# Experts' shares by broadcast transfers instead of selector matmuls, in a two-layer attention and mixture-of-experts kernel

## The chip, the cores and the metric

The kernel runs on one core of one Trainium2 chip. The metric is the device time of one launch in microseconds (us); lower is better. A core has five engines that each work through a queue of their own, in order: TensorE (PE, matmuls; PEld is its weight load), VectorE (DVE), ScalarE (ACT), GpSimd (POOL) and SyncE (SP, which here only issues DMAs). They wait for each other by semaphores. The on-chip memory has 128 partitions; a matmul's result lands in one of 8 PSUM banks, which only PE, DVE and ACT reach. All data are fp32.

## The reference, cut to what matters

The input `x` is 64 batches of 128 rows of 128 numbers. Four layers are added to it one after the other: an attention over 248 keys, a mixture of 8 experts of which each row uses two (its "FFN" of layer 0), a second attention over 120 keys, and a second mixture. The change is in the second mixture, which is computed for all 8 experts and then weighted:

```python
logits = xf @ Wg.T + bg                                   # [rows, 8]
top_gates, top_idx = jax.lax.top_k(logits, 2)
top_gates = jax.nn.softmax(top_gates, axis=-1)            # the two shares of a row
h = jax.nn.gelu(einsum('nd,erd->enr', xf, W1), approximate=False)   # R = 64 per expert
eout = 2.0 * einsum('enr,edr->ned', h, W2)
out = sum(top_gates[:, :, None] * take(eout, top_idx))    # added to x
```

A row's output is thus the sum over the experts of share times `h W2`, where six of the eight shares are zero. The kernel multiplies `h` by the share before it multiplies by `W2`.

## The kernel before

The work is in groups of `GB` = 4 batches, 16 groups in all. The launch has three stages: the first attention with the first router beside it (to about 640 us), the first mixture's tiles (to about 955 us), and the second attention with the second mixture beside it (to the end). The change touches the last stage.

In the second attention, `attention(1, ...)`, one pass of the loop at L553 handles one batch `it`, each step for a batch that is further back. A pass does, in this order (L595 to L612): the values of batch `it-3` (L475) and their copy `ov` (L484); the rounds (L442), which hold the maxima of batch `it` (one matmul per bank at L407, reduced on DVE at L414) and the scores of batch `it-2` (L430) with their exponentials on ACT (L438); then one piece of the experts (`aside.piece`); then the preparation of the next group (`prep`); the output steps `out3`, `out2`, `out4` (L504, L491 with DVE's L495 and L497, L511); the shift of batch `it-1` (transposes at L459, then DVE's L462, which the scores of the next pass need); `out5` (L516) and the statistics for the last norm (L112, L113); and the gathers on POOL for later batches (L1364, L1376). Within one engine this written order is kept: PE, ACT, DVE and POOL are scheduled by hand (`ORDERED`, L16). SP is not in that set in this stage: its order is the scheduler's.

The preparation of group g+1 is spread over the four passes of group g (L354): keys (`prep_k`, L202 and L207) and then `prep_heads` in pass 1, values (`prep_v`, L214 and L221) and the norm's transposes (`prep_x`) in pass 2, queries (`prep_q`, L292 with ACT's L295 and L301) in pass 3. `prep_heads` (L309 to L315) is four DVE multiplications of 128x480 (L313) which make, from the keys, the copies `k4` that the next group's maxima read.

The experts of one group are a generator, `experts` (L1408), of four pieces, so that one piece goes into each pass. Piece 1 (in the pass where `prep_v` stands too) turns the shares of four batches (`gates`, 32 columns per batch of which 8 are used) with one transpose (L1417) and copies the result to `gT` on ACT (L1419); then, for each of four chunks c of two experts each, a matmul into a bank (L1424) and a Gelu on ACT into `hT` (L1427). Piece 2 makes, by 16 matmuls with a constant `select` (L1434; the hardware runs each as two passes, so 32 in the records), the shares of each batch spread over the 128 rows of a chunk, in four banks, and multiplies `hT` by them on DVE (L1439, four instructions, one per batch). Pieces 3 and 4 multiply by `W2` (L1445) and add to `x` (L1450); after piece 4 SP writes the group out (L1452). The exponentials of attention and Gelu need different function tables on ACT; each change of function costs an ACT_TABLE_LOAD, put ahead of the first instruction that needs it.

After the last batch `aside.rest` (L1464) runs the pieces that are left, with nothing of attention beside them: that part is called the tail here.

Of the kernel before, what the change touches and what calls it, by code (L numbers as in the profile page):

```python
# [8 lines left out]
F32 = mybir.dt.float32  # L9
I32 = mybir.dt.int32  # L10
AF = mybir.ActivationFunctionType
ALU = mybir.AluOpType
# [6 lines left out]
GB = 4  # L19
NG = B // GB  # L20
S = 128
# [7 lines left out]
E = 8  # L29
# [15 lines left out]
def transformer_kernel(ctx, tc, a, out):  # L45
    nc = tc.nc

    const = ctx.enter_context(tc.tile_pool(name="const", bufs=1))
# [4 lines left out]
    for g in range(NG):  # L53
        t = resid.tile([S, GB, D], F32, name=f"x_{g}", tag=f"x_{g}")
# [17 lines left out]
    def load_const(name, shape, src):  # L72
        t = const.tile(shape, F32, name=f"c_{name}", tag=f"c_{name}")
        nc.sync.dma_start(t, src)
        return t
# [109 lines left out]
    for s in range(2):  # L185
        k = keep.tile([128, NV, GB, KF + KC], F32, name=f"k2_{s}", tag=f"k2_{s}")
# [14 lines left out]
    def keys_of(w, src, g, n0, pk):  # L201
        nc.tensor.matmul(  # L202
            pk[:, : GB * n0], lhsT=w["wk"], rhs=src.rearrange("d b k -> d (b k)"),
            start=True, stop=True,
        )
        for v in range(NV):
            nc.scalar.activation(  # L207
                K2[g % 2][:, v, :, 0:n0], pk[:, : GB * n0].rearrange("p (b k) -> p b k", b=GB),
                AF.Identity, bias=w["bk"][:, v : v + 1], scale=kmask[:, v : v + 1],
            )  # L210
# [21 lines left out]
    def attention(layer, w, norm, first, aside):  # L232
# [5 lines left out]
        with ExitStack() as es:  # L238
# [37 lines left out]
            def mtile():  # L276
                return banks.tile([128, 512], F32, name="bank", tag="bank")

            def prep_x(g):
                xnT = work.tile([D, GB * S], F32, name="xnT", tag="xnT", bufs=1)  # L280
                norm.turned(normed.pop(g), mtile(), xnT)
                xnTs[g] = xnT
                q4s[g] = work.tile([128, GB, NS, S], F32, name="q4", tag="q4", bufs=3 if first else 2)
                if not first:
                    qfs[g] = work.tile([128, GB, S], F32, name="qf", tag="qf")
# [20 lines left out]
            def prep_k(g):  # L306
                keys_of(w, src[g], g, n0, mtile())

            def prep_heads(g):  # L309

                k4s[g] = work.tile([128, NS, GB, KC], F32, name="k4", tag="k4")
                for s in range(NS):
                    nc.vector.tensor_scalar(  # L313
                        k4s[g][:, s], k2[g % 2][:, s // 2], hmask[:, s : s + 1], None, ALU.mult
                    )  # L315

            def prep_v(g):
                values_of(w, src[g], g, n0, mtile())
# [20 lines left out]
            def prep(it, half):  # L339

                g, j = it // GB + 1, it % GB
                if not first:
                    if g == 1:
                        if (j, half) == (0, 0):
                            prep_k(1)
                            prep_v(1)
                        elif (j, half) == (0, 1):
                            prep_x(1)
                        elif j == 1:
                            prep_q(1, half)  # L350
                            if half:
                                prep_heads(1)
                    elif g < NG:
                        pieces = (  # L354
                            (), (lambda: prep_k(g), lambda: prep_heads(g)),
                            (lambda: prep_v(g), lambda: prep_x(g)),
                            (lambda: prep_q(g, 0), lambda: prep_q(g, 1)),
                        )[j]
                        if half < len(pieces):
                            pieces[half]()  # L360
                    return
                if half == 0 and it < GB - 1:
                    prep_batch(it + 1)
                if (it, half) == (0, 1):
                    prep_v(0)
                    norm_of(1)
                if (it, half) == (1, 1):
                    biased(0)
                if (it, half) == (2, 1):
                    prep_x(1)  # L370
                if (it, half) == (3, 0):
                    prep_q(1, 0)
                    prep_q(1, 1)
                if (j, half) == (3, 1):
                    if g + 1 < NG:
                        prep_x(g + 1)
                elif g >= NG:
                    return
                elif j == 0 and it:
                    prep_q(g, half)  # L380
                elif (j, half) == (2, 0):
                    prep_v(g)
                elif (j, half) == (2, 1):
                    prep_k(g)
# [134 lines left out]
            def norm_of(g):  # L519
                if g < NG:  # L520
                    normed[g] = norm.normed(g)
                    biased(g)
# [262 lines left out]
    hbm = ctx.enter_context(tc.tile_pool(name="hbm", bufs=1, space=bass.MemoryType.DRAM))  # L785
    xs = hbm.tile([E * CAP, ROW], F32, name="xs", tag="xs")
    ys = hbm.tile([NTL * TT, D], F32, name="ys", tag="ys")
    place = ctx.enter_context(tc.tile_pool(name="place", bufs=1))
    at = place.tile([S, B, 2], I32, name="at", tag="at")
    posns = place.tile([S, 2, B], F32, name="posns", tag="posns")  # L790
# [536 lines left out]
    nc.sync.dma_start(row_number, a["row_number"])  # L1327
    steps256 = load_row("steps256", CAP // TT)
    tiles = load_const("tiles", [1, NA], a["tiles"])
    select = load_const("select", [128, 4, 128], a["select"])  # L1330
    lw2 = load_const("lw2T", [128, 4, D], a["lw2T"].rearrange("(c p) d -> p c d", p=128))
    with tc.manual_schedule(engines=ORDERED):
        for _ in range(B - 2):
# [8 lines left out]
    class Aside1:  # L1342
# [65 lines left out]
        def experts(self):  # L1408


            for g in range(NG):
                while not self.ready:
                    yield
                of, gates = self.ready.pop(0)
                assert of == g
                pt = self.mtile()[:, :S]
                nc.tensor.transpose(pt, gates.rearrange("p b e -> p (b e)"), ident)  # L1417
                gT = self.pool.tile([128, S], F32, name="gT", tag="gT", bufs=1)
                nc.scalar.copy(gT, pt)  # L1419
                xnT = self.xnTs.pop(g)  # L1420
                hT = self.pool.tile([128, 4, GB * S], F32, name="h1", tag="h1", bufs=1)
                for c in range(4):
                    ph = self.mtile()
                    nc.tensor.matmul(  # L1424
                        ph, lhsT=lw1[:, c * 128 : (c + 1) * 128], rhs=xnT, start=True, stop=True
                    )
                    nc.scalar.activation(hT[:, c, :], ph, AF.Gelu)  # L1427
                yield

                pg = [self.mtile().rearrange("p (c t) -> p c t", c=4) for _ in range(GB)]  # L1430
                for c in range(4):
                    for j in range(GB):
                        r = slice(32 * j, 32 * j + 32)
                        nc.tensor.matmul(  # L1434
                            pg[j][:, c, :], lhsT=select[r, c, :], rhs=gT[r, :], start=True, stop=True
                        )
                for j in range(GB):
                    h = hT[:, :, j * S : (j + 1) * S]
                    nc.vector.tensor_tensor(h, h, pg[j], ALU.mult)  # L1439
                yield  # L1440
                for j0 in range(0, GB, 2):
                    po = self.mtile()[:, : 2 * D].rearrange("p (j d) -> p j d", j=2)
                    for j in range(2):
                        for c in range(4):
                            nc.tensor.matmul(  # L1445
                                po[:, j, :], lhsT=hT[:, c, (j0 + j) * S : (j0 + j + 1) * S],
                                rhs=lw2[:, c, :], start=(c == 0), stop=(c == 3),
                            )
                    x = xg[g][:, j0 : j0 + 2, :]
                    nc.vector.tensor_tensor(x, x, po, ALU.add)  # L1450
                    if j0:
                        nc.sync.dma_start(  # L1452
                            out[g * GB : (g + 1) * GB].rearrange("b p d -> p b d"), xg[g]
                        )
                    yield
# [21 lines left out]
def _laid_out(inp):  # L1477
# [17 lines left out]
    o = {"x": A["x"]}  # L1495
    o["fsideT"] = A["fside_BxSxS_0"].transpose(2, 0, 1)
    c = A["ctx_1024"]
    o["ctxT"] = c.transpose(2, 0, 1)
    k = moved(c.reshape(B * KC, D)).reshape(B, KC, 1, D)
# [32 lines left out]
    o["upper"] = np.triu(np.ones((128, 128), np.float32), 1)  # L1532
    o["ones"] = np.ones((128, 128), np.float32)
    o["steps256"] = np.arange(CAP // TT, dtype=np.float32) * TT

    t = np.zeros((4, 32, 4, 2, 64), np.float32)
    for e in range(E):
        t[:, e, e // 2, e % 2, :] = 1.0
    o["select"] = t.reshape(128, 4, 128)
    o["tiles"] = np.arange(NA, dtype=np.float32).reshape(1, -1)  # L1540
    o["row_number"] = np.arange(1, 129, dtype=np.float32).reshape(-1, 1)
    o["first_row"] = np.arange(E, dtype=np.float32) * CAP
# [23 lines left out]
```

## Time and profile before

| what | us |
|---|---|
| median of 3 runs (lowest, highest) | 1522.33 (1518.69, 1523.64) |
| the profiled execution, its own time | 1516.1 |
| its span, from the first instruction to the last | 1514.3 |
| PE busy in the span | 1421.0 (94%) |
| DVE busy | 1102.4 (73%) |
| ACT busy | 847.6 (56%) |
| POOL busy | 640.4 (42%) |
| second attention with its experts: first expert matmul (L1424) of groups 0, 11 and 12 | 1071.0, 1435.9, 1461.5 |
| the same of groups 13, 14, 15 (the tail) | 1479.9, 1491.2, 1500.5 |

From group 0 to group 11 a group takes (1435.9 - 1071.0) / 11 = 33.2 us; groups with the router's steps for a pair of groups take about 34.4, the ones between 32.0.

How to read the views: times are counted from the start of the span. A timeline row is start, duration, engine, line, operation, output<-inputs, shapes and count, and in square brackets the engine's idle time before it and what released it. A row of the chain of waits is start, duration, and what the end of the launch was waiting for in that stretch. A row of the windows view gives, for one stretch, its length, each engine's busy time and number of instructions, then the clock granted to TensorE (1 is full), the busy share of the DMA engines, and the GB/s that they moved. PE's busy time is modelled and holds waits inside a group of matmuls.

### The profile page before, as it was taken

The page shows a single profiled execution, that of the slowest core. Times are in us where ns is not written, and L with a number is a line of the kernel's source. Part 1 is how long each engine was busy: PE and PEld are TensorE (multiplying, and loading weights), DVE is VectorE, ACT ScalarE, POOL GpSimd, SP SyncE. Part 2 cuts the span into 40 slices and gives each one's busy share as a digit, 9 for nine tenths or more (in the row PEclk, how much of TensorE's full clock was granted, in tenths as well). Part 3 has the DMA queues.
Part 4 walks back from the last instruction along what each step waited for, and adds up shares of the span by engine and source line. Part 5 has one row for each costly group of instructions (what it writes and reads, how often), then busy time and mean ns, then how long its engine had stood idle before and what let it go on. Part 6 is the DMA issues. An engine that isn't in the chain of part 4 may idle for free.

```text
span 1514.3 us, 42033 instructions
## 1 busy us (share of the span) xinstructions
PE 1421.0 (94%) x16620; PEld 1107.5 (73%) x16620; DVE 1102.4 (73%) x3024; ACT 847.6 (56%) x1740; POOL 640.4 (42%) x1195
## 2 busy tenths in 40 slices
PE   7999999999999999888999999898999999999987
PEld 5777777777777677777888888566666776767665
DVE  6777888888888988455754444687777778787763
ACT  4666666666666666543333333566667566666643
POOL 4123254646465635654001122377546555454210
PEclk9999999999999999999999999899999999999999
DMA  8433333333222221366766667111011111100000
GB/s 201 120 80 80 79 82 96 89 93 94 63 66 60 58 73 40 107 184 202 214 197 199 201 195 205 49 34 34 22 36 29 39 35 32 31 29 23 8 16 22
DMA packets 143719, 133.03 MB, mean 88 GB/s; under 512 B 48546, under 2 KB 126114, under 8 KB 141602
## 3 DMA queue, kind: packets, MB, share of 16 engines
q1 hardware_dynamic: 135330, 113.02, 27.3%
q0 software_dynamic: 8192, 17.32, 3.7%
q8 instruction: 132, 2.16, 0.6%
q14 instruction: 65, 0.53, 0.1%
HBM read 97.32 MB, written 32.97 MB: 86 GB/s over the span
## 4 chain that ended last, share of the span: by engine, by line
PE 69%; DVE 15%; DMA 4%; POOL 4%; ACT 4%; issue 2%; SPq 1%; POOLq 0%; DVEq 0%; ACTq 0%
PE bank L430 11%; PE bank L394 10%; PE bank L475 9%; PE bank L1115 9%; PE bank L1424 4%; PE bank L1445 4%; DVE nm L414 4%; PE bank L1128 3%; DMA q<-xs 2%; PE bank L407 2%; PE bank L214 2%; DVE q L462 2%; PE bank L511 2%; PE bank L681 2%; PE bank L202 2%
## 5 line engine op out<-in xcount | busy, mean ns | idle before, releaser
L414 DVE TENSOR_REDUCE nm<-bank 128x2 f32<-128x496 f32 (+1 forms) x768 | 463.5, 662 | 77.6 <-PE bank L430 61.8
L438 ACT ACTIVATE p<-bank 120x512 f32<-120x512 f32 (+1 forms) x768 | 402.1, 605 | 126.8 <-PE bank L430 123.9
L430 PE MATMUL bank<-q,k 32*120 32x256 f32 (+1 forms) x3072 | 438.1, 399 | 11.4 <-DVE nm L414 5.2
L430 PEld LDWEIGHTS bank<-q,k 32*120 32x120 f32 (+1 forms) x3072 | 293.5, 181 | 56.8 <-DVE nm L414 17.3
L394 PE MATMUL bank<-k,q 32*128 32x248 f32 x2048 | 291.0, 399 | 0.7 <-ACT q L334 0.5
L394 PEld LDWEIGHTS bank<-k,q 32*128 32x128 f32 x2048 | 202.2, 189 | 47.9 <-issue 11.0
L1120 DVE TENSOR_TENSOR p<-p,bank 128x256 f32<-128x256 f32 x213 | 88.0, 420 | 121.0 <-ACT p L1119 120.5
L475 PE MATMUL bank<-p,v 128*32 128x128 f32 (+1 forms) x4096 | 175.6, 275 | 0.2
L407 PE MATMUL bank<-k,qf 32*128 32x480 f32 x512 | 153.8, 602 | 0.8 <-ACT qf L295 0.8
L807 POOL DMA_INDIRECT xs<-xn,at x128 | 129.2, 1009 | 27.9 <-issue 24.3
L1119 ACT ACTIVATE p<-bank 128x256 f32<-128x256 f32 x213 | 81.0, 384 | 98.9 <-PE bank L1115 97.9
L484 ACT COPY ov<-bank 128x256 f32<-128x256 f32 x128 | 48.1, 376 | 143.5 <-PE bank L475 143.4
L475 PEld LDWEIGHTS bank<-p,v 128*32 128x32 f32 (+1 forms) x4096 | 108.8, 109 | 22.8 <-issue 13.7
L1364 POOL DMA_INDIRECT yb<-ys,back x112 | 108.5, 969 | 27.7 <-issue 19.5
L1115 PE MATMUL bank<-q 128*128 128x256 f32 x516 | 118.6, 379 | 1.6 <-ACT q L1106 1.6
L462 DVE SCALAR_TENSOR_TENSOR q<-bank,c_smask,q 128x256 f32<-128x256 f32 x256 | 111.1, 475 | 8.2 <-PE bank L459 7.8
L167 POOL TENSOR_SCALAR xn<-x,mv,rstd 128x128 f32<-128x128 f32 x252 | 110.2, 449 | 7.5 <-issue 1.4
L1115 PEld LDWEIGHTS bank<-q 128*128 128x128 f32 x516 | 94.7, 190 | 13.0 <-ACT q L1106 1.9
L475 PE MATMUL bank<-p,vc 120*32 120x128 f32 x2048 | 103.2, 272 | 0.0
L155 POOL TENSOR_SCALAR rstd<-mv 128x4 f32<-128x4 f32 x32 | 6.3, 198 | 219.9 <-DVE mv L113 123.0
L301 ACT ACTIVATE q<-bank,c_a_bq,c_hmask 128x512 f32<-128x512 f32 x124 | 90.1, 789 | 9.8 <-PE bank L292 9.8
L1157 POOL DMA_INDIRECT kvT<-ys,back x16 | 15.4, 961 | 189.7 <-DMA vc<-xs 114.0
(224 smaller groups left out, 2465.7 us busy)
## 6 DMA issues: line engine op xcount, KB each, us to landing
q<-in_w SPq DMA_DIRECT2D x43, 576.0 KB
vc<-in_w SPq DMA_DIRECT2D x28, 576.0 KB
vc<-in_ctx_v SPq DMA_DIRECT2D x16, 960.0 KB
ys<-zero SPq DMA_DIRECT2D x71, 128.0 KB
k<-in_ctx_k SPq DMA_DIRECT2D x32, 240.0 KB
q<-xs SPq DMA_DIRECT2D x43, 128.0 KB
ys<-q SPq DMA_DIRECT2D x43, 128.0 KB
x<-in_x SPq DMA_DIRECT2D x16, 256.0 KB
```

Of the source, the lines that this page charges most:

```text
L167: nc.gpsimd.tensor_scalar(xn[:, j, :D], xg[g][:, j, :], self.mv[:, b, 0:1], self.rstd[:, b : b + 1], ALU.add, ALU.mult,)
L301: nc.scalar.activation(q4s[g][:, :, s, :], pq.rearrange("p (b q) -> p b q", b=GB), AF.Identity, bias=w["bq"][:, s : s + 1], scale=hmask[:, ...
L394: nc.tensor.matmul(pa[:, u, :], lhsT=q4s[g][r, j, s, :], rhs=k2[g % 2][r, s // 2, j, :], start=True, stop=True,)
L407: lambda: nc.tensor.matmul(pa, lhsT=qfs[g][r, j, :], rhs=k4s[g][r, :, j, :], start=True, stop=True),
L414: nc.vector.tensor_reduce(nm[b % 2].rearrange("q i (a s) -> q a i s", s=16)[:, 2 * ra + v : 2 * ra + v + len(slots) // 2, :, 0], pa.rearra ...
L430: nc.tensor.matmul(pb[:n, v * 256 : (v + 1) * 256], lhsT=k2[g % 2][r, v, j, k0 : k0 + n], rhs=q4s[g][r, j, 2 * v : 2 * v + 2, :].rearrange ...
L438: nc.scalar.activation(ps_[b][:n, c, ra, :], pb[:n], AF.Exp, scale=SCALE)
L462: nc.vector.scalar_tensor_tensor(q, pm, smask[:, v : v + 1], q, ALU.mult, ALU.add)
L475: nc.tensor.matmul(pav[32 * ra : 32 * ra + 32, v * S : (v + 1) * S], lhsT=vs[g % 2][c][:, j, 4 * v + ra, i, :], rhs=p[:n, c, ra, (2 * v + ...
L807: s = nc.gpsimd.indirect_dma_start(xs, bass.IndirectOffsetOnAxis(at[:, j, k : k + 1], 0), xn, None)
L1115: nc.tensor.matmul(ph[:, u, :], lhsT=w[:, c, u * 128 : (u + 1) * 128], rhs=xT, start=True, stop=True)
L1364: nc.gpsimd.indirect_dma_start(y[:, k, b % 2, :], None, ys, bass.IndirectOffsetOnAxis(back[:, b, k : k + 1], 0),)
```

## The change

The shares are no longer made by matmuls. `gT` becomes a part of a new tile `share` (128 x 4 x 512); after the copy on ACT, SP writes its 4 x 8 used rows of 512 B each to a scratch in HBM (`shares_`, [8 experts, 4 batches, 128], two of them in turn), and two further DMAs read it back, each to 64 partitions: every one of these partitions gets, for each chunk c, the 2 KB row of one expert (256 pieces of 2 KB per DMA, 512 KB; together 1 MB). `hT` is then multiplied by `share` chunk by chunk: chunks 0 and 1 on GpSimd, 2 and 3 on VectorE. An exponential of one element, to no use in the result, follows the Gelus on ACT. The constant `select` and its load go. `prep_heads` moves from the second half of pass 1 to just ahead of `prep_v` in pass 2, where it stands behind that pass's maxima in DVE's queue.

```diff
@@ prep, groups from 2 on
                         pieces = (
-                            (), (lambda: prep_k(g), lambda: prep_heads(g)),
-                            (lambda: prep_v(g), lambda: prep_x(g)),
+                            (), (lambda: prep_k(g),),
+                            (lambda: (prep_heads(g), prep_v(g)), lambda: prep_x(g)),
                             (lambda: prep_q(g, 0), lambda: prep_q(g, 1)),
                         )[j]
@@
+    shares_ = [hbm.tile([E, GB, S], F32, name=f"shares_{k}", tag=f"shares_{k}") for k in range(2)]
@@
-    select = load_const("select", [128, 4, 128], a["select"])
+    again = const.tile([1, 2], F32, name="again", tag="again")
+    nc.vector.memset(again, 0.0)
@@ experts
-                gT = self.pool.tile([128, S], F32, name="gT", tag="gT", bufs=1)
+                share = self.pool.tile([128, 4, GB * S], F32, name="share", tag="share", bufs=1)
+                gT = share[:, 3, :S]
                 nc.scalar.copy(gT, pt)
+                there = shares_[g % 2]
+                for j in range(GB):
+                    nc.sync.dma_start(there[:, j, :], gT[32 * j : 32 * j + E, :])
+                for i in range(2):
+                    nc.sync.dma_start(
+                        share[64 * i : 64 * i + 64],
+                        there.rearrange("(c i) j t -> i c (j t)", i=2)[i]
+                        .unsqueeze(0).to_broadcast([64, 4, GB * S]),
+                    )
...
                     nc.scalar.activation(hT[:, c, :], ph, AF.Gelu)
+                nc.scalar.activation(again[:, 1:2], again[:, 0:1], AF.Exp)
                 yield
-                pg = [self.mtile().rearrange("p (c t) -> p c t", c=4) for _ in range(GB)]
                 for c in range(4):
-                    for j in range(GB):
-                        r = slice(32 * j, 32 * j + 32)
-                        nc.tensor.matmul(
-                            pg[j][:, c, :], lhsT=select[r, c, :], rhs=gT[r, :], start=True, stop=True
-                        )
-                for j in range(GB):
-                    h = hT[:, :, j * S : (j + 1) * S]
-                    nc.vector.tensor_tensor(h, h, pg[j], ALU.mult)
+                    (nc.gpsimd if c < 2 else nc.vector).tensor_tensor(
+                        hT[:, c, :], hT[:, c, :], share[:, c, :], ALU.mult
+                    )
                 yield
```

In the changed program SP's queue holds, for a group of the first nine: the four writes; the load of the keys' source `kvT` for a later group (L256), which waits for PE's values of this pass (L214); the two reads; and the output of an older group. From group 9 on there is no `kvT` between. For the last two groups the output of the group before stands behind the first of the four writes. On POOL the two multiplications stand between the gathers of two passes, on DVE where L1439 stood.

More of the change, by code (lines that the diff above doesn't have):

```diff
@@ L1534, in _laid_out @@
     o["steps256"] = np.arange(CAP // TT, dtype=np.float32) * TT
[L1536 to L1539, printed above, removed]
     o["tiles"] = np.arange(NA, dtype=np.float32).reshape(1, -1)
```

## The prediction

> **What bounds the kernel now.** I read the busy table first (PE 94%, but PE's busy time is modelled and holds waits), then the chain of waits in the last stage, which says what was waited for. Two neighbouring groups, cut to the rows that the change touches (start, us, what):
>
> ```profile
> 1178.40 1.28 ACT L438
> 1179.70 0.61 ACT p L438
> 1180.35 1.02 PE bank L1434 x24
> 1181.42 2.48 DVE h L1439 x4
> ...
> 1198.86 1.52 DVE k L313 x4
> ...
> 1212.84 1.28 ACT L438
> 1214.14 0.61 ACT p L438
> 1214.79 1.16 PE bank L1434 x28
> 1215.95 1.06 PE bank L292 x2
> ...
> 1231.38 1.51 DVE k L313 x4
> ```
>
> The first group (1169.5 to 1204.0, 34.4 us, with the router's steps) goes through the table load of ACT, the exponential, the selector matmuls and the four multiplications, and from there to the next L1424 it stays mostly with DVE; L313 is on it. The second (32.0 us) leaves DVE after L1434 and runs along PE; L313 comes back only near the end. So the change works on pieces that do set the end, in both kinds of group. The timeline gives the moments between which the new transfers must fit:
>
> ```profile
> 1170.07 0.30 ACT L1419 COPY gT<-bank 128x128 f32<-128x128 f32 x1
> ...
> 1174.12 0.33 SPq L256 DMA_DIRECT2D kvT<-in_ctxT  x1
> 1174.13 0.76 DVE L221 TENSOR_TENSOR v<-bank,c_a_bv 120x256 f32<-120x256 f32 x2 [3.54 <-PE bank L214]
> ...
> 1178.22 2.35 DVE L414 TENSOR_REDUCE nm<-bank 128x4 f32<-128x480 f32 x4
> ...
> 1181.42 2.48 DVE L1439 TENSOR_TENSOR h<-h,bank 128x512 f32<-128x512 f32 x4 [0.85 <-PE bank L1434]
> ```
>
> Call T the end of the copy to `gT`: 1170.37, and 1204.31 in the second group. DVE is ready to multiply at 1180.57 = T+10.2 (second group 1214.98 = T+10.7), and its next instruction starts at 1183.82 (1218.26).
>
> **The transfers (not in the trace before).** SP issues one DMA per 0.47 us (the first loads: 3.20, 3.67, 4.14), and data move about 0.6 us after the issue. So: four writes issued to T+2.0, landed about T+2.9; then the load of `kvT` at T+3.75 stands ahead of the reads (it waits for PE's L214); reads issued to T+5.0; their data from about T+6.0, behind those of `kvT`. The share is there at T+6.0+D+0.1, D being the data time of 1 MB. The nearest rows (length, then busy times; the last columns are clock, DMA share, GB/s):
>
> ```profile
> 6.30:7.50 1.20, 1.20 (x2) 0.23 (x1) 0.34 (x2) 0.00 (x0) 0.75 (x1) 1.00 1.13 324
> 32.10:34.20 2.10, 2.10 (x30) 1.77 (x32) 1.09 (x3) 0.39 (x2) 0.66 (x1) 0.73 0.26 59
> 1175.00:1176.50 1.50, 1.50 (x26) 1.33 (x30) 0.85 (x4) 0.54 (x1) 1.47 (x2) 1.00 0.75 213
> ```
>
> 324 GB/s is the best stretch (a load of keys): D = 3.2. 59 GB/s is a constant's 512 B row sent to 128 partitions, the only rows of that kind: D = 17.8. 213 GB/s is `kvT`, in pieces of 1,920 B, nearly the 2 KB of the new ones: D = 4.9, which I take, since the size of the piece is what the new transfer shares with it. The share then lands at T+11.0, and at T+9.05 where no `kvT` stands between (groups 9 to 11: reads issued from T+2.9, data from T+4.05).
>
> The Trainium skill ("SBUF — State Buffer", section "Door 1: The DMA port swizzle") says that a transfer to partitions 0 to 63 reaches only half of the ports, 196 GB/s measured for 1 MiB. By it D would be an estimated 5.3, which speaks against halving the partitions; no transfer here goes to 64 of them.
>
> **The multiplications.** Rows: SBUF by SBUF on DVE 0.68 us (L1012, 128x512), on POOL 1.27 (L526, same size). Two each: DVE 1.36 alone; 3.9 if its two stand behind POOL's two (2.54); L313 takes 0.46 alone and up to 0.68 beside POOL's L167, so they do disturb each other. I take one POOL instruction between DVE's two, 2.6, and for POOL 3.2.
>
> The Trainium skill (same page, "SBUF: two separate sides") calls the port pair of the two engines an exclusive lock, also for a VectorE operation with two SBUF inputs against a GpSimd one that reads SBUF. The L313 row agrees with a disturbance, not yet with a full block; the page's end would be 3.9, some 18 us more over the launch than my 2.6.
>
> **Per group in attention.** The multiplication ended at 1183.82. First kind: 1181.37 + 2.6 = 1183.97, +0.15; L313 off its place, -1.5 (in its new place DVE idles 3.5 us ahead of L221, so it costs nothing there; if PE's L214 came 2 us earlier it would): -1.35. Second kind: 1215.31 + 2.6 = 1217.9 against 1218.26, -0.35, and -1.5, since PE, which set this group's end, loses the table load and the selector matmuls (1.28 + 1.16 = 2.4): -1.85. Mean -1.6 in nine groups; in groups 9 to 11, where the share is there before DVE asks, -2.15. Sum -20.9. Three uses of L313 before the first experts: -2. The exponential's table load now stands behind the Gelus, ahead of need; its cover is some 3 us in which ACT waits for PE. POOL idles 7.1 us later in the pass (L155), so its 3.2 and its wait move gathers that have room: 0 taken, 0.5 a group (6) if that room is gone. The constant's removed load and the memset: 0.
>
> **Group 12 and the tail.** Group 12 (`gT` at 1462.1, no `kvT`): share 1471.1, DVE done 1473.7 against 1470.1: +3.6, and 0.9 for POOL, whose multiplications now stand ahead of the last norm (1473.4): +4.5. In the tail nothing of attention lies beside the transfer:
>
> ```profile
> 1480.00:1484.00 4.00, 4.00 (x6) 1.54 (x5) 1.14 (x6) 2.40 (x4) 0.00 (x0) 0.51 0.00 0
> ...
> 1491.18 3.60 PE L1424 MATMUL bank<-xnT,c_lw1T 128*128 128x512 f32 x8
> 1494.71 1.17 PE L1434 MATMUL bank<-gT,c_select 32*128 32x128 f32 x32
> 1496.71 3.84 PE L1445 MATMUL bank<-c_lw2T,h 128*128 128x128 f32 x32 [0.83 <-DVE h L1439]
> ```
>
> A tail group took 9.32 us (1491.07 to 1500.39, from transpose to transpose; 11.46 the first, 9.5 the last). Now: transpose and copy 0.63, share 4.05 + 4.9 + 0.1 = 9.05 (reads issued right behind the writes), 0.1, POOL 3.2, L1445 3.6, 0.1, and a colder PE: after about 3 us without work the clock of L1424 was 0.51 and its eight took 5.61 instead of 3.60, so +2.0 on L1445 (0 to 3.84). Sum 18.7, and 19.1 where an output stands between SP's writes: +7.2, +9.8, +9.6 = +26.6.
>
> **Sum**: -20.9 - 2 + 4.5 + 26.6 = +8.2. The profiled execution took 1516.1 (span 1514.3), so 1524.3; the median of the runs is 1522.33, 6.2 above it: **1530.5**. What the attention gains, the tail gives back.
>
> **Rivals.**
> *A, faster: the share is there when DVE asks, and the two engines don't block each other.* D = 4.1 (256 GB/s) and 1.36 us: first kind ends 1.9 earlier, with L313 -3.4; second kind held by PE at -2.4; 12 groups -34.7, -2, group 12 +2.5, tail +22.2: -12, 1510. From one side alone it decides at D under 4.1 (slope 13 us per us: nine groups, group 12, three tail groups) or at a multiplication under 1.9. For it: 324 GB/s was moved, DVE's 0.68 row. Against it: `kvT` never kept 324 over its transfer, L313's row.
> *B, the reads run like the constants' broadcast.* All pieces come from eight rows of HBM, as there from one. At 59 GB/s, D = 17.8: 12.9 x 13 + 11.5 x 3 (groups 9 to 11) on top, 1734; at 118 GB/s, D = 8.9, 52 + 8 more: 1591. For it: the only broadcast in the trace. Against: pieces of 512 B, and DMA engines busy 26% there, so few bytes per piece may be what made it slow.
> *POOL becomes the bound:* 3.2 us in each group against 7.1 of idle time; at worst 6 us, inside the range. That the table load would stay on the path is excluded by the order: it follows the Gelus there.
>
> **Chances.** Forecast 0.50 (its own range 1518 to 1560: D from 4.1 to 6.5, multiplications from 1.9 to 3.9), A 0.27, B 0.23. The range reaches to A's 1505 (PE's end a little lower than I hold) and B's milder end, 1600. About 0.3% (4.6 us) is what can be told from no change. Faster: A nearly whole, 0.25, and a little of the forecast, 0.05: 0.30. Same: 0.12 of the forecast and A's rest. Slower: 0.58.
>
> **What the profile after would show.** Right: reads landing 10.5 to 11.5 us after the copy; DVE waiting about 0.8 us for them in the first kind; a period of 31 to 32; no ACT table load in the chain ahead of L438; L313 in DVE's idle time before `v`; tail groups near 19 with clock near half on L1445. Wrong: a landing beyond T+13 (B), before T+10.2 (A), multiplications of DVE longer than 2.6 from start to end, or a period that does not fall although DVE ends earlier, since PE then has a bound of its own.

## The result, and the profile after

| | before | changed |
|---|---|---|
| median of 4 runs (lowest to highest), us | 1520.51 (1517.61 to 1523.64) | 1584.83 (1582.58 to 1594.57) |
| span of the profiled execution | 1514.3 | 1585.0 |
| start of the experts to the end (from the first `gT`) | 442.9 | 513.3 |
| groups 0 to 8 | 299.9 | 330.9 |
| groups 9 to 11 | 90.8 | 93.3 |
| group 12 | 18.3 | 24.8 |
| tail, groups 13 to 15 | 33.9 | 64.3 |

The ratio is 1.043, with an interval of 1.0404 to 1.0455. The rows of groups are differences between the ends of the copies to `gT` (L1422 in the changed kernel); the sum forecast -14.4, -6.5, +4.5 and +26.6 for the last four, and -2 ahead of them. So group 12 and the tail came nearly as worked out; the nine groups with `kvT` are 31 us longer instead of 14 shorter, and groups 9 to 11 are 2.5 longer instead of 6.5 shorter.

One of the nine, timeline of the changed kernel (T is 1182.10):

```profile
1181.80 0.30 ACT L1422 COPY share<-bank 128x128 f32<-128x128 f32 x1
1182.12 1.30 SPq L1426 DMA_DIRECT2D shares<-share  x4
1185.53 0.36 SPq L256 DMA_DIRECT2D kvT<-in_ctxT  x1
1186.12 1.24 SPq L1428 DMA_DIRECT2D share<-shares  x2
...
1196.12 0.69 DVE L1445 TENSOR_TENSOR h<-h,share 128x512 f32<-128x512 f32 x1 [4.15 <-DMA share<-shares]
1196.16 1.77 POOL L1445 TENSOR_TENSOR h<-h,share 128x512 f32<-128x512 f32 x1 [4.91 <-DMA share<-shares]
...
1196.73 1.75 DVE L1445 TENSOR_TENSOR h<-h,share 128x512 f32<-128x512 f32 x1
...
1197.89 1.71 POOL L1445 TENSOR_TENSOR h<-h,share 128x512 f32<-128x512 f32 x1
```

The reads are issued from T+4.0 to T+5.3, near the sum's T+5.0, but DVE starts at T+14.0 and not T+11.0: it stood 4.15 us. The chain of waits goes through this transfer for 9.3 us:

```profile
1186.75 9.29 DMA share<-shares
```

The windows view (length; busy times of PE, PEld, DVE, ACT, POOL; clock, DMA share, GB/s) shows the read itself, then what the wait does to PE, then a read in the tail:

```profile
1188.00:1195.50 7.50, 6.27 (x90) 3.99 (x79) 3.86 (x12) 6.05 (x12) 2.72 (x4) 1.00 0.79 165
1194.30:1199.50 5.20, 0.00 (x0) 0.00 (x0) 3.35 (x7) 1.27 (x3) 3.34 (x2) 0.77 0.05 10
1199.50:1203.60 4.10, 4.06 (x23) 2.89 (x23) 3.89 (x13) 1.08 (x2) 3.53 (x5) 0.50 0.14 34
...
1545.50:1549.50 4.00, 0.00 (x0) 0.00 (x0) 0.00 (x0) 0.05 (x1) 0.00 (x0) 0.90 1.02 230
```

In attention the read keeps 165 GB/s with the gathers' transfers among it, and its packets run from 1187.7 to 1195.5, 7.8 us, the longest of the nine (6.5 to 7.8, mean 7.0); in the tail they run 5.1 us. PE has nothing for 5.2 us, since the scores (L430) need DVE's L462, which stands behind the multiplications; and when they come, PE works at a clock of 0.50 for 4 us. The waits from 1071 to 1402 (in all, times, longest) and the tail's timeline:

```profile
PEld bank L430 <- DVE q L462: 49.0, 9, 6.0
...
DVE h L1445 <- DMA share<-shares: 25.5, 7, 4.2
```

```profile
1540.05 0.27 ACT L1422 COPY share<-bank 128x128 f32<-128x128 f32 x1 [4.12 <-PE bank L1419]
...
1543.60 1.24 SPq L1428 DMA_DIRECT2D share<-shares  x2
1551.22 3.44 POOL L1445 TENSOR_TENSOR h<-h,share 128x512 f32<-128x512 f32 x2 [17.05 <-DMA share<-shares]
...
1554.72 5.62 PE L1453 MATMUL bank<-c_lw2T,h 128*128 128x128 f32 x30 [0.88 <-POOL h L1445]
```

5.62 us for thirty L1453 (two more had run ahead of them), where the sum had 3.6 + 2.0; GpSimd 3.44, where it had 3.2. The release came late: the last packet ended at 1550.3, and the multiplications start 0.9 us after it; over all groups this gap is 0.6 to 1.1 us.

### The profile page after: what moved, and what is told of

Its sections match the earlier page's. It is cut to its first block, busy times and chain, and to the rows that moved or that the text cites. A ratio compares the mean times of both kernels' runs of the same rounds, so it can differ in the third digit from the quotient of the medians.

```text
span 1585.0 us, 41284 instructions
## 1 busy us (share of the span) xinstructions
PE 1420.2 (90%) x16108; PEld 1109.0 (70%) x16108; DVE 1116.5 (70%) x2993; ACT 852.1 (54%) x1759; POOL 701.0 (44%) x1227
## 4 chain that ended last, share of the span: by engine, by line
PE 65%; DVE 13%; DMA 11%; POOL 4%; ACT 2%; issue 2%; SPq 1%; POOLq 0%; ACTq 0%; DVEq 0%
PE bank L430 11%; PE bank L394 9%; PE bank L1116 8%; PE bank L475 8%; DMA share<-shares 6%; PE bank L1453 5%; DVE nm L414 4%; PE bank L1129 3%; PE bank L407 3%; PE bank L1437 2%; DMA q<-xs 2%; PE bank L214 2%; DVE h L1445 2%; DMA vc<-xs 2%; PE bank L202 2%
## 5 line engine op out<-in xcount | busy, mean ns | idle before, releaser
L430 PE MATMUL bank<-q,k 32*120 32x256 f32 (+1 forms) x3072 | 454.0, 413 | 60.0 <-DVE q L462 53.1
L430 PEld LDWEIGHTS bank<-q,k 32*120 32x120 f32 (+1 forms) x3072 | 307.5, 188 | 104.3 <-DVE q L462 65.0
L407 PE MATMUL bank<-k,qf 32*128 32x480 f32 x512 | 168.7, 654 | 0.8 <-ACT qf L295 0.8
L1453 PE MATMUL bank<-c_lw2T,h 128*128 128x128 f32 x512 | 82.6, 326 | 44.7 <-POOL h L1445 37.6
L1453 PEld LDWEIGHTS bank<-c_lw2T,h 128*128 128x128 f32 x512 | 75.8, 234 | 63.4 <-POOL h L1445 41.5
L167 POOL TENSOR_SCALAR xn<-x,mv,rstd 128x128 f32<-128x128 f32 x252 | 114.2, 466 | 7.5 <-issue 1.4
L462 DVE SCALAR_TENSOR_TENSOR q<-bank,c_smask,q 128x256 f32<-128x256 f32 x256 | 111.0, 475 | 6.9 <-PE bank L459 6.5
L1445 POOL TENSOR_TENSOR h<-h,share 128x512 f32<-128x512 f32 x32 | 54.5, 1724 | 129.1 <-DMA share<-shares 110.7
```

The costliest lines, as they stand in the source:

```text
L167: nc.gpsimd.tensor_scalar(xn[:, j, :D], xg[g][:, j, :], self.mv[:, b, 0:1], self.rstd[:, b : b + 1], ALU.add, ALU.mult,)
L407: lambda: nc.tensor.matmul(pa, lhsT=qfs[g][r, j, :], rhs=k4s[g][r, :, j, :], start=True, stop=True),
L430: nc.tensor.matmul(pb[:n, v * 256 : (v + 1) * 256], lhsT=k2[g % 2][r, v, j, k0 : k0 + n], rhs=q4s[g][r, j, 2 * v : 2 * v + 2, :].rearrange ...
L462: nc.vector.scalar_tensor_tensor(q, pm, smask[:, v : v + 1], q, ALU.mult, ALU.add)
L1453: nc.tensor.matmul(po[:, j, :], lhsT=hT[:, c, (j0 + j) * S : (j0 + j + 1) * S], rhs=lw2[:, c, :], start=(c == 0), stop=(c == 3),)
```

## The experiments

My theory after the result: the transfers land late, the clock falls in the wait, and what does not touch the shares gains as worked out. The rival: the two engines' multiplications are what costs. The runs were made on several chips, and the chip matters: the kernel before took 1576 on the one of e5 to e8 and 1574 on the one of e9 to e12, but 1519 to 1520 on those of e1 to e4, of e13 to e16 and of e17 and e18. I call these the slower and the faster chips. So e5 to e8 and e10 to e12 are set against the changed kernel on a slower chip (e9; for e5 to e8 it is the other of the two), and times of groups only against such from chips of the same pace.

**e1, e2, e3: the parts without the shares.** Edits to the kernel before; e1 has the first, e2 the second, e3 both:

```diff
-    (), (lambda: prep_k(g), lambda: prep_heads(g)),
-    (lambda: prep_v(g), lambda: prep_x(g)),
+    (), (lambda: prep_k(g),),
+    (lambda: (prep_heads(g), prep_v(g)), lambda: prep_x(g)),
```

```diff
     nc.scalar.activation(hT[:, c, :], ph, AF.Gelu)
+nc.scalar.activation(again[:, 1:2], again[:, 0:1], AF.Exp)
```

> The kernel before with one part of the change alone: the heads' keys (L313) are made ahead of the values in pass 2. My theory: the parts that do not touch the shares gain what the sum gave them, and the loss lies in the transfers. Then this gains 1.5 us in each group with the router's steps and 0.6 to 1.5 in the others, 12 to 18 in all: 1502 to 1509. Rival: attention is held by something else (PE's own length), and L313 only moves the wait: within 5 of 1520.

> The kernel before with another part alone: the exponential of one element behind the Gelus, so that the table load leaves the wait. My theory: DVE waited 0.85 us ahead of the multiplications for PE, which waited for ACT; groups with the router's steps gain 0.85, the others up to 1.28: 10 to 13 in all, 1507 to 1511. Rival: the earlier load only lengthens ACT's queue, within 5 of 1520.

> The kernel before with the two parts together, shares still made by selector matmuls. My theory: the gains add up, since one lies ahead of the multiplications and one behind them: 22 to 31, 1489 to 1498. Rival (PE is the bound of a group): no more than the larger of the two alone.

Measured, beside 1519.35 for the kernel before: 1502.94 (ratio 0.989, 0.986 to 0.991), 1509.14 (0.992, 0.990 to 0.995) and 1495.69 (0.983, 0.980 to 0.986). All three lie in the theory's ranges, and nearly add up. So two parts of the change are worth 24 us, and the shares cost 89.

**e4: no transport.** `self.still` is filled once with 0.25.

```diff
-    share = self.pool.tile([128, 4, GB * S], F32, name="share", ...)
+    share = self.still
...
-    nc.sync.dma_start(there[:, j, :], gT[32 * j : 32 * j + E, :])
-    nc.sync.dma_start(share[64 * i : 64 * i + 64], ...)
```

> The changed kernel without the transport: no writes and no reads of the shares; the tile of shares is filled once with a constant, so the output lacks the real shares. Multiplications, their engines and the order stay. My theory (the loss is the wait for the transfers and the clock that falls in it): groups in attention about 2 us under those of before, the tail groups about 2 us over: 1495 to 1510. Rival (the multiplications on two engines disturb each other, and PE waits for GpSimd's): stays over 1560.

Measured 1501.83 (0.989, 0.985 to 0.992). The rival fell as an explanation of the loss: with both engines multiplying as in the change, 83 of its us are gone with the transport. But groups 0 to 8 took 293.9 us here, where the theory had some 282, and 283.8 with the selector matmuls in their old place (e16); e17 goes after that. One cause shows in the multiplications. A group of e4 in which GpSimd begins first, cut together from DVE's and GpSimd's timelines:

```profile
1106.62 1.28 POOL L1437 TENSOR_TENSOR h<-h,share 128x512 f32<-128x512 f32 x1
1107.21 2.47 DVE L1437 TENSOR_TENSOR h<-h,share 128x512 f32<-128x512 f32 x1
1107.84 1.28 POOL L1437 TENSOR_TENSOR h<-h,share 128x512 f32<-128x512 f32 x1
...
1109.61 0.68 DVE L1437 TENSOR_TENSOR h<-h,share 128x512 f32<-128x512 f32 x1
```

GpSimd's two take no longer than alone, one right behind the other, and DVE's first, started beside them, ends only 0.56 us after GpSimd's second: it was held all the while. In the changed kernel, where both start together, they take turns: 0.69, then 1.77, 1.75 and 1.71, each but the first longer by about as much as was left of the other engine's one.

**e5: `kvT` off SP's queue.**

```diff
-    nc.sync.dma_start(t, a["fsideT" if first else "ctxT"][...])
+    (nc.sync if first else nc.scalar).dma_start(t, a[...][...])
```

> The changed kernel, with the loads of kvT in the second attention issued from ACT's queue at the start of a group's first pass instead of from SP between the writes and the reads. My theory: that load holds the reads back by about 1.7 us and its data another 1, and with the clock that falls in the wait it makes the nine groups 3.4 us longer; without it they run like groups 9 to 11 (32.4 us): 1550 to 1558. Rival (GpSimd's gathers slow the reads, whatever stands on SP): little of it comes back, over 1570.

1594.76 (1.013 of before, 1.009 to 1.016), against 1619.74 for e9: 25 less. Its groups 0 to 8 took 304.9 us against 336.2, and their reads 5.2 to 6.9 us (mean 5.8) against 5.4 to 7.5 (6.9), begun 2 us earlier. The theory's numbers were for a faster chip; as a difference it had 27 to 35, a little more than came.

**e6, e7: reads to all partitions, two repeats outermost.**

```diff
-    for i in range(2):
-        nc.sync.dma_start(share[64 * i : 64 * i + 64], ...)
+    for c in range(4):
+        nc.sync.dma_start(
+            share[:, c, :],
+            there.rearrange("(c i) j t -> i c (j t)", i=2)[:, c]
+            .unsqueeze(1).to_broadcast([2, 64, GB * S]),
+        )
```

> The changed kernel, with the share read back by four DMAs of one chunk each to all 128 partitions (256 KB each, the same 2 KB pieces) instead of two DMAs to 64 partitions each; kvT stays between. My theory: a piece took 84 ns at the head of the read and 171 ns once all 16 DMA engines wrote to one half of the partitions, so with both halves open 1 MB takes near 3 us alone instead of 5.0: tail groups 2 us shorter, groups in attention 2 to 3.5 (clock included): 1548 to 1565. Rival (eight rows of HBM or the gathers are what slows the pieces): 1580 to 1587.

> Both edits of the two runs before this one. My theory: the share lands before DVE asks in all groups of attention, which then run as with no transport (about 2 us under before each), and only the tail and group 12 are left as loss (about +20): 1512 to 1528. Rivals: as the better one of the two alone, 1550 or more, if only one of the two was the cause.

1831.98 and 1831.68 (both 1.162 of before): far on the other side of every expectation. The windows view of e6 within a read:

```profile
1210.00:1216.00 6.00, 1.31 (x14) 0.33 (x6) 0.00 (x0) 2.36 (x5) 1.87 (x2) 0.74 0.13 51
```

A DMA share of 0.13 is two of 16 engines, and 51 GB/s is 25 pieces of 2 KB in a us, each 84 ns long in the records: the pieces were quick, but only two engines had any. The step that stands outermost in this read has two repeats, in the change's own read 64. These two runs say nothing on the halves of the partitions.

**e8: PE kept busy.**

```diff
+    for _ in range(5 if g < 9 else 10 if g > 11 else 0):
+        nc.tensor.matmul(self.mtile(), lhsT=lw1[:, :128], rhs=xnT, start=True, stop=True)
     for c in range(4):
         (nc.gpsimd if c < 2 else nc.vector).tensor_tensor(...)
```

> The changed kernel with matmuls that nobody reads (five of 128x512 in groups 0 to 8, none in 9 to 11, ten from group 12 on) behind the L1437 matmuls' pass, so that PE is not idle while DVE waits for the share. The transfers are unchanged. My theory: of the 3.4 us that a group lost, 1.5 to 1.8 is PE running at half clock after the wait, and about 2 us of each tail group: 1560 to 1568. Rival (the whole loss is the wait itself): 1583 to 1600, the matmuls only adding.

1608.62 against 1619.74: 11 less, though PE does more; the theory had 17 to 25 less and the rival none. Groups 0 to 8 took 326.2 us against 336.2, with a granted clock of 0.99 against 0.90, while DVE started as late as before (T+13.4 to T+14.9, in e9 T+12.9 to T+14.8). The clock is shown as a cause, with 1.1 us a group, net of the added matmuls, instead of the 1.5 to 1.8 that I expected. From the first `gT` on, the profile of e8 is 19 us shorter; ahead of it, where nothing was edited, 7 longer, so the 11 hold a difference between the two chips or executions too.

**e9 and e10: the changed kernel on a slower chip, and the second read on ACT's queue.**

```diff
+    read(nc.sync, 0)
...
     nc.scalar.activation(again[:, 1:2], again[:, 0:1], AF.Exp)
+    read(nc.scalar, 1)
```

> The changed kernel once more, as it is, beside the three of this call, because the kernel before took 1575 in the call before this one against 1520 in the others, and its numbers have to be set against the changed kernel of the same chip: 1.04 of the kernel before.

> The changed kernel with the second of the two reads (to partitions 64 to 127) issued from ACT's queue behind the Gelus instead of from SP; sizes and pieces stay. My theory: a read to 64 partitions is held by that half, 171 ns a piece, so the two halves written at the same time take near 3 us instead of 5.0, and one of them passes kvT: tail groups 2 us shorter, attention's 2 to 3: 25 to 35 less than the changed kernel beside it. Rival (eight rows of HBM set the pace): within 8 of it.

e9: 1619.74, 1.029 of before (1.027 to 1.030), where the faster chip gave 1.043. e10: 1601.22, 18.5 less, all of it in attention: groups 0 to 8 took 312.2 us against 336.2, the tail 65.6 against 63.2. In attention the two reads hardly met: ACT's had passed `kvT` and was nearly done (1166.6 to 1170.1 in one group) when SP's began at 1169.7. In the tail they were issued at the same moment (1548.19 on SP, 1548.20 on ACT), and still their packets ran one after the other, SP's from 1549.6 to 1552.3 and ACT's from 1551.6 to 1554.8, 5.2 us in all. So two queues did not get the two halves written at the same time, and e10's gain is most likely that of passing `kvT`.

**e11: experts in turn over the partitions.** W1 and W2 are laid out to match; same bytes, same 2 KB pieces.

```diff
-    for i in range(2):
-        nc.sync.dma_start(share[64 * i : 64 * i + 64], ...)
+    for c in range(4):
+        nc.sync.dma_start(
+            share[:, c, :],
+            there[2 * c : 2 * c + 2].rearrange("i j t -> i (j t)")
+            .unsqueeze(0).to_broadcast([64, 2, GB * S]),
+        )
```

> The changed kernel with each chunk's two experts laid in turn over even and odd partitions (the weights W1 and W2 are laid out to match), so that a read of one chunk goes to all 128 partitions in 2 KB pieces with 64 repeats as its outermost step, four DMAs of 256 KB. In the run with four DMAs of two repeats of 64 only 25 pieces came per us, each still 84 ns long, so about two DMA engines worked; my theory for that run is that a DMA is dealt to the engines by its outermost step. Then here all engines work, to both halves: 1 MB in 3 us, 20 to 35 less than the changed kernel beside it. Rival 1 (128 partitions in one DMA is what was slow): 1800 or more. Rival 2 (eight rows of HBM set the pace of the pieces): within 8 of the changed kernel.

1549.19 (0.984 of before, 0.982 to 0.985): 70.5 less than e9, twice what I expected. Rival 1 fell, and with it the doubt on e6: 128 partitions are quick when 64 repeats stand outermost. Rival 2 fell too, since the same eight rows of HBM are read. Within a read, and the multiplications by kind (busy, mean ns, idle before):

```profile
1202.50:1205.00 2.50, 2.35 (x25) 1.38 (x18) 2.43 (x9) 1.09 (x2) 2.17 (x3) 1.00 0.99 324
```

```profile
L1445 POOL TENSOR_TENSOR h<-h,share 128x512 f32<-128x512 f32 x32 | 40.1, 1271 | 59.9 <-DMA share<-shares 52.1 <-ACT oT L506 7.5
L1445 DVE TENSOR_TENSOR h<-h,share 128x512 f32<-128x512 f32 x32 | 28.4, 925 | 27.1 <-DMA share<-shares 26.5 <-ACT p L438 0.5
```

The nearest stretch of the changed kernel, with its DMA engines as busy:

```profile
1189.00:1194.00 5.00, 5.00 (x65) 3.21 (x58) 2.91 (x8) 4.23 (x10) 1.91 (x2) 1.00 0.97 200
```

324 GB/s instead of 200. Pieces took 84 ns (median in every group), where the changed kernel's took 84 in the first microsecond of a read and mostly 115 to 180 after it. The whole read of 1 MB is shortened by less, since its four DMAs are issued one after the other: 4.3 to 5.2 us in groups 0 to 8 against 5.4 to 7.5 in e9, and 4.0 to 4.3 in the tail against 5.1 to 5.4. Since the chunks land one after the other, GpSimd also starts before DVE: 1,271 and 925 ns a multiplication, against 1,708 and 1,265 in e9.

**e12: selector matmuls back in groups 12 to 15.**

```diff
+TAIL = 12
...
+    if g == TAIL:
+        nc.sync.dma_start(share[:, 0, :].rearrange("p (c m) -> p c m", c=4), a["select"])
...
+    if g < TAIL:
         for c in range(4):
             (nc.gpsimd if c < 2 else nc.vector).tensor_tensor(...)
+    else:
...
+        nc.tensor.matmul(pg[j][:, c, :], lhsT=select[r, c, :], rhs=gT[r, :], ...)
...
+        nc.vector.tensor_tensor(h, h, pg[j], ALU.mult)
```

> The changed kernel up to group 11; groups 12 to 15 make their shares with the selector matmuls and multiply on DVE as before the change (the selector is loaded into the tile of the shares, which is free then). My theory: group 12 and the tail are half of the loss, 36: 34 to 38 less than the changed kernel beside it. Rival (the end is late because of what attention left behind): under 15 less.

1585.30: 34.4 less than e9, in the theory's range. Tail 33.0 us against 63.1, group 12 18.5 against 24.9.

**e13: the order of landing alone.**

```diff
-    for i in range(2):
-        nc.sync.dma_start(share[64 * i : 64 * i + 64], ...)
+    for h in range(2):
+        for i in range(2):
+            nc.sync.dma_start(share[64 * i : 64 * i + 64, 2 * h : 2 * h + 2, :], ...)
```

> The changed kernel with each of its two reads cut in two by chunks, in the order chunks 0 and 1 of both halves of the partitions, then chunks 2 and 3 of both: GpSimd's half lands first, but every DMA still goes to 64 partitions. My theory for the 70 us that the spread layout gained: most of it is the pace (171 ns a piece when one half is written, 84 when both are), a smaller part that GpSimd and DVE no longer start together (1.7 and 1.2 us a multiplication, 1.27 and 0.68 apart): here pieces stay at 171 ns, and 15 to 30 less than the changed kernel (1.029 of before where before takes 1574). Rival (the order of landing is all of the gain): 55 to 75 less.

On a faster chip: 1557.61 (1.025, 1.022 to 1.029), 27 less than the changed kernel's 1584.83, in the theory's range. Pieces took 112 to 148 ns (medians of the groups), far from e11's 84. Its multiplications:

```profile
L1446 POOL TENSOR_TENSOR h<-h,share 128x512 f32<-128x512 f32 x32 | 39.9, 1268 | 82.5 <-DMA share<-shares 73.6 <-ACT ov L484 5.1 <-ACT qf L295 2.5
L1446 DVE TENSOR_TENSOR h<-h,share 128x512 f32<-128x512 f32 x32 | 24.0, 790 | 58.7 <-DMA share<-shares 58.7
```

1,268 and 790 ns, where the changed kernel had 1,724 and 1,244. So the common landing cost 27 of the 70 or so. In the rest two things are together that no run takes apart: the pace of a read to one half, and e11's landing in four steps instead of two. The two figures are also from different chips, so the split is rough.

**e14, e15, e16: can the transfers be made to pay?** e14 is e11 with e12's edit, e15 adds e5's, e16 is e3 again beside them.

> The spread layout with the selector matmuls back in groups 12 to 15. My theory: its four last groups were 20 us longer than those of the run with the tail undone, so 1529 where before takes 1574 (0.97 of before). Rival (the two edits share their gain): 1540 or more.

> The same with kvT loaded from ACT's queue. My theory: DVE still waited up to 1.4 us between its two multiplications in groups 0 to 8 for the last chunk, since kvT stood ahead; without it 5 to 12 less than the run beside it. Rival (what is left is not the transfer's): within 4 of it.

> Once more the kernel before with the moved keys and the early table load and no transfers, beside the spread layout's best: which of the two ways is better. 0.983 of before. My theory: the spread layout with the tail undone is better by 1% or more, since it takes the selector matmuls from PE and 1.1 us of multiplication from DVE in each group. Rival: equal, attention being bound by what both leave alone.

1507.08 (0.992, 0.989 to 0.994), 1511.52 (0.995, 0.993 to 0.997) and 1495.91 (0.986, 0.984 to 0.989). All three theories fell (e14 came out as its rival had it: the two edits share their gain): the best form of the transfers beats the kernel before and loses to the kernel with the two other parts and no transfers at all, by 11 us; and with the pace right, `kvT` on SP costs nothing that shows. Groups 0 to 8: 296.0, 297.1 and 283.8 us.

**e17, e18: all multiplications on DVE**, without transport (e4's edit) and with e14's.

```diff
-    (nc.gpsimd if c < 2 else nc.vector).tensor_tensor(
+    nc.vector.tensor_tensor(
```

> The run without transport (shares filled once with a constant, so the output lacks the real ones) with all four multiplications on DVE. My theory: there DVE's two multiplications took 3.0 us because GpSimd's, started just ahead, held its first one for 2.1; four of 0.68 on DVE alone take 2.7, and PE no longer waits for GpSimd, so groups with the router's steps fall from 33.4 or 35.2 to about 33, the others stay at 30.5: groups 0 to 8 take 285 to 290 us instead of 293.9, in the tail nothing changes: 0.982 to 0.987 of before. Rival (GpSimd takes work off DVE, as the change would have it): slower than with GpSimd, 0.99 or more.

> The spread layout with the selector matmuls back in groups 12 to 15 and all four multiplications on DVE. My theory: with the transfers landing chunk by chunk DVE multiplies chunks 0 and 1 while 2 and 3 are on their way, so it gains little or nothing over the run with GpSimd (0.992 of before): 0.985 to 0.995, and the kernel before with the two other parts alone (0.983 to 0.986) stays the best. Rival (without GpSimd in it the transfers pay): 0.98 or less.

1510.86 (0.994, 0.992 to 0.996) and 1510.36 (0.994, 0.991 to 0.996). The theory of e17 fell: groups 0 to 8 took 299.9 us, more than with GpSimd (293.9). Four multiplications on DVE took 3.33 us where I had 2.7: they are held by GpSimd's additions of gathered rows too (1.37 us for one that began beside such an addition; mean 848 ns, not 680). The four from PSUM before the change took 2.48, each between 677 and 689 ns, beside GpSimd's additions as well. The theory of e18 held. And PE waits again. Windows of e17 (a stretch behind that wait, then its groups 0 to 8) and of e16 (groups 0 to 8):

```profile
1114.60:1118.20 3.60, 3.56 (x23) 2.72 (x23) 3.32 (x12) 1.08 (x2) 1.62 (x2) 0.53 0.14 36
...
1067.00:1360.00 293.00, 262.43 (x2811) 196.41 (x2812) 244.52 (x666) 187.58 (x366) 169.99 (x239) 0.95 0.12 32
```

```profile
1068.00:1352.00 284.00, 272.36 (x3179) 207.32 (x3178) 240.28 (x687) 191.92 (x377) 167.53 (x245) 1.00 0.13 35
```

With no selector matmuls PE's clock was 0.95 (0.97 in e4), with them 1.00. It is not their absence as such that lowers it. Groups 0, 1 and 3 of e4:

```profile
1066.92:1097.42 30.50, 29.92 (x324) 22.02 (x323) 25.34 (x65) 21.33 (x42) 21.21 (x30) 1.00 0.12 35
1097.42:1130.79 33.37, 29.82 (x320) 22.23 (x319) 28.05 (x83) 21.32 (x42) 21.75 (x30) 0.95 0.11 32
1161.32:1196.49 35.17, 31.48 (x320) 23.58 (x319) 28.14 (x83) 21.40 (x42) 21.76 (x30) 0.90 0.11 31
```

Groups 0, 2, 4 and 6 kept the full clock and took 30.5, less than e16's 30.8. Groups 1, 3, 5 and 7 are those in which DVE was held as shown above; PE stood 1.8 us for the scores in each, and then got half its clock for 3.4 us (1 and 5) or 6.8 (3 and 7). By the rows that is an estimated 1.7 (0.05 x 33.4) and 3.5 us (0.10 x 35.2) of PE's time; they took 1.4 and 3.2 more than e16's 32.0. In e17 PE stood 2.1 to 2.3 us in every group, and 0.05 x 293 us is an estimated 15 of the 16 that it is longer. So the chain is most likely: DVE held by GpSimd, PE waiting for DVE, the clock falling in that wait. No run here changes the clock alone; e8 does so in the changed kernel.

## Why the prediction was wrong

- **What bounds the kernel**: right. The two parts that were read off the chain, the moved keys and the table load, gave 24 us (e3), in the size of the sum's -20.9 - 2. I had them as gains that the change keeps; that the changed kernel had them too, under the wait, is argued and not shown.
- **The transfers**: here the sum failed. The share was to be there at T+11.0; in the nine groups DVE's multiplications started at T+13.6 to T+14.2 (mean 13.8), and in groups 9 to 11 at T+10.1 to T+10.6 instead of T+9.05. Data began to move at T+5.9 in the mean, as summed. Two terms were too small. "D = 4.9, which I take" was right for a read alone (5.1 us in the tail) and wrong in the nine groups, where it measured 7.0 in the mean; and the 0.1 from landing to start measured 0.9. I had divided 1 MB by the rate of a transfer to 120 partitions, and counted nothing beside it. In the read shown 0.24 MB of other transfers went with the 1 MB, GpSimd's gathers nearly all; at the tail's rate that is an estimated 1.2 us, but no run takes the gathers away. Nor was it the size of the piece that mattered: pieces of 2 KB took 84 ns in e11 and 112 to 168 (medians of the groups) in the changed kernel and e13, which differ from it in the partitions that a read goes to.
- The Trainium skill ("SBUF — State Buffer", section "Door 1: The DMA port swizzle") gives 196 GB/s for 1 MiB to partitions 0 to 63. The runs agree: 1 MB in 5.1 us in the tail, 206 GB/s, against 324 in a stretch of e11's read to all partitions. By the page alone D would have been an estimated 5.3 and not 7.0; the gathers in the same stretch are what neither the row nor the page's figure counts.
- **The multiplications**: right in size, 2.36 and 3.44 for 2.6 and 3.2, but the disturbance was taken as a mild one. Where GpSimd begins first, as in e4, DVE waits for both of its instructions and takes 3.08 for its two, where I had let one of GpSimd's come between.
- The skill's exclusive lock (same page, "SBUF: two separate sides") is what the rows of e4 show: DVE was held over the whole of GpSimd's instruction. It would take 3.90 for the four (1.36 + 2.54); they were over in 3.5, which does not speak against it, since two multiplications of one engine follow each other in 0.60 us on DVE and 1.22 on GpSimd, less than the 0.68 and 1.27 that each is long, so by these steps the four need an estimated 3.6.
- **The wait's price**: counted once, paid twice. I gave the fall of the clock to the tail (+2.0, measured 2.0) and put it at nothing in attention, though a wait of DVE there leaves PE without work as well: 5.2 us idle in the group shown, then half clock, 1.1 us a group by e8. Of the 5.0 us by which one of the nine groups missed the sum (+3.4 for -1.6), 4.1 went with the transport (330.9 against e4's 293.9) and 0.9 stayed without it.
- **Group 12 and the tail**: +4.5 and +26.6 against +6.5 and +30.4. What is missing in the tail is mostly the 0.85 us from the last packet to the start of the multiplications, where I had 0.1 (2.3 of the 3.8), and the output between SP's writes, which put the reads of the last two groups off by 0.9 instead of 0.4.
- **The rivals**: B had the right side, and 118 GB/s as its milder end gave 1591, near the 1584.83, but for the wrong reason, so its nearness is luck; it blamed the eight rows of HBM, and e11 reads the same rows at 324 GB/s. (Its full price adds up to 1733, not 1734.) The sign that I had named for B, a landing beyond T+13, is thus no sign of its cause. A's condition, the share there when DVE asks, is nearly met in e14 (DVE stood 4 us for it in the whole launch), and groups 0 to 8 still took 296.0 us against 299.9, a gain of 0.4 us a group where A had 2.9: A's 1.36 us for the multiplications was not to be had beside GpSimd.

## What to carry to other kernels

Before a transfer takes the place of matmuls, ask whether those matmuls stood on the path or beside it: here they cost PE 1.0 to 1.2 us a group, and the wait for the transfers left it idle for 4 to 5. A multiplication that moves from a PSUM operand to two in SBUF, beside work on GpSimd, has to be priced with GpSimd's whole instruction in front of it. A transfer's rate has to be taken from a row to the same partitions and under the same company, and a wait of a few us in front of PE has to be priced with the slow stretch behind it. A bundle of edits is best taken apart: two of three parts here were worth 1.6%, and the third cost 6%.

## What the runs showed of the hardware

- Reads to 64 partitions moved 2 KB pieces at medians of 125 to 168 ns, one to all 128 at 84 ns: with the DMA engines 0.97 and 0.99 busy, 200 GB/s against 324. 1 MB with nothing beside it took 5.1 us by two reads of 64 partitions and 4.0 to 4.3 by four of 128.
- Two reads to the two halves, issued within 0.01 us on two queues, ran one after the other, 5.2 us for both (e10's tail).
- A read whose outermost step had two repeats ran on about two of the 16 DMA engines (51 GB/s, share 0.13); with 64 repeats outermost, on all (0.99).
- From the last packet of a read to the start of the waiting multiplication 0.6 to 1.1 us passed in the changed kernel.
- Multiplications of 128x512 from SBUF took 1.27 us on GpSimd and 0.68 on DVE apart, 1.72 and 1.24 when started together; one of DVE's that began beside GpSimd's first took 2.47 and ended after GpSimd's second. DVE's from PSUM took 0.68 also beside GpSimd's work.
- After PE had stood 1.8 us (e4) to 5.3 us (the changed kernel), its granted clock was mostly 0.50 for 3.4, 6.8 or 10.2 us; two waits of 2.1 us in e17 passed without it.
- Two chips took 1574 and 1576 us for the kernel before and three others 1519 to 1520, and the changed kernel stood at 1.029 on one of the two instead of 1.043. The changed kernel was 35 us longer there, 28 of them ahead of the experts; why, the runs do not show.
